# A linear-attention and RWKV block: another order at the start, for the woven tiles and between the two parts

## The chip, the cores and the metric

The kernel runs on one core of a Trainium2 chip. The metric is the device time of one execution in microseconds, as the median of several runs. A core has TensorE (PE in the profile), VectorE (DVE), ScalarE (ACT), GpSimd (POOL) and SyncE (SP), each with an instruction stream of its own that it works through in order; they wait for each other through semaphores. SP does nothing here but issue DMAs. ScalarE issues some as well.

## What is computed

The input x has 16 sequences of 1024 rows with 512 columns, in float32. The block has two parts, each with a residual and a layer norm:

```python
x = layernorm(x + attention(x)); x = layernorm(x + ffn(x))
# attention: 16 heads of 32
q, k, v = split(x @ Wqkv.T + bqkv)
qf, kf = relu(rope(rmsnorm(q, gq))), relu(rope(rmsnorm(k, gk)))
vk  = einsum('bhlp,bhld->bhpd', [v, 1], kf)      # a sum over a whole sequence
res = einsum('bhpd,bhld->bhlp', vk, qf)
out = rmsnorm((res[..., :-1] / (res[..., -1:] + eps)) @ Wout.T + bout, gout)
# ffn: x_prev is x shifted down one row within the sequence
r = sigmoid((mu_r*x + (1-mu_r)*x_prev) @ W_r.T)
k = square(relu((mu_k*x + (1-mu_k)*x_prev) @ W_k.T))
out = r * (k @ W_v.T)
```

The q side of a row can be finished only when vk of its sequence is known.

## The kernel before

Work goes by tiles of 128 rows: N = 128 tiles, eight to a sequence. Every float32 operand of a product is split into a rounded high part (a copy on ScalarE) and the rest (a subtraction on VectorE or GpSimd), and each product is three matmuls: high by high, high by low, low by high. A tile's projection to q is therefore 12 matmuls of 128x512 (four chunks of 512 by three).

**First part.** `slot(i)` (L566) is called for i = 0 to N-1. It issues the load of xt two tiles ahead (L568), the projections of tile i to q and k (`proj`, L367), the splits of the next tile (`split_x`, `split_xn`), the product of k and x of the tile before (`add_kx`, L452, 12 matmuls into four PSUM banks that gather a whole sequence), `rope` (L420: VectorE multiplies both projections by tables, ScalarE sums their squares, POOL takes the root at L120, then k is rectified and split), the tables for the next tile (`tables`, L397: POOL makes the first eight tiles' tables from g_qk, cos and sin and SP stores them; later tiles load them), and `seed` (L385: ScalarE copies the bias into the PSUM banks of the next projections). PSUM has eight banks: four gather k and x, and four are handed out in turn by `bank` (L96) to everything else, so a new user of a bank waits for the fourth user before it.

Once in eight slots a sequence is closed: `finish_a` (copies the four banks out), `finish_s` (column sums of k), `finish_b` (products with the v weights, 16 + 16 small matmuls, then the mask), `finish_c` (product with Wout, which gives a matrix m for the sequence that is stored as m_d). In slots i with i mod 8 = 1 stand finish_a and finish_s, in 2 finish_b, in 3 to 6 one finish_c each.

**Woven tiles.** The first NPRE = 7 tiles' q side is taken into the first part: from slot FIRST = 40, one tile every STEP = 8 slots. In slot FIRST + 8j the tile's q and x are loaded (the first one also the matrix m of its sequence); `part_s` (L217) seeds its bank with the output bias. One slot later come `part_q` (L189, six VectorE operations that normalise q), and for the first NT = 4 tiles `part_qt` (transposes q on TensorE and splits it), `part_m` (product with m, 12 matmuls) and `part_y` (L245: norms and residual on VectorE, ScalarE and POOL).

**Late weights.** `late_weight` (L553) loads one of 20 blocks of weights, splits it and, for the second part's weights, stores the halves. The code calls it once a slot from slot 1, but nothing ties it there.

**Between the parts** (L685 to L728): the first mixes of the second part, the q side of tiles 4 to 6, the closing of the last sequence, weights' loads and the q side of tiles 7 and 8. **Second part** (L781): for each half sequence s (four tiles), `part_t` transposes and mixes, `part_fk`, `part_fr` and `part_fv` are the three products, and the q side of later tiles is taken in, one each u.

**What sets the order.** The program's order is not the order on the engines. The framework (`TileContext(..., schedule_with_timeline_sim=True)`, L878) plans each engine's order by a simulation of its own: what it takes to be ready goes first, and the program's order breaks ties. `tc.issue_after(ins)` holds what is issued in its block on the same engine behind `ins`; it waits for nothing. Memory comes from pools; a pool that is opened after another was closed takes its memory and waits for the last use of what it overlaps.

Of the kernel before, what the change touches and what calls it, by code (L numbers as in the profile page):

```python
# [15 lines left out]
P = 128  # L16
# [6 lines left out]
FIRST, STEP = 40, 8  # L23
# [10 lines left out]
def kernel(  # L34
# [70 lines left out]
    const.tile([P, 40], F32, name="fill_const")  # L105
    tp.tile([P, 56], F32, name="fill_top")
    halo = const.tile([P, NC_], F32, name="halo")
    ident = const.tile([P, P], F32, name="ident")
    make_identity(nc, ident)
    rstd_all = const.tile([P, N, 2], F32, name="rstd_all")  # L110
# [146 lines left out]


    with ExitStack() as a_ctx:
# [50 lines left out]

        m0 = te.tile([P, 2, DIM], F32R, tag="m", bufs=2, name="m0")
        V.memset(f32(m0[:, 0, :]), 0.0)
        for n in range(8):
            T.matmul(bank(f"pswarm{n}"), lhsT=m0[:, 0, 0:P], rhs=m0[:, 0, :], start=True, stop=True)
        load_xt(0)
        split_x(0)
        b_qk = ca.tile([P, 2 * DIM], F32, name="b_qk")
        nc.scalar.dma_start(out=b_qk, in_=bqkv[0 : 2 * DIM].partition_broadcast(P))
        for j in range(2):
            cols = slice(j * DIM, (j + 1) * DIM)  # L320
            for c in range(NC_):
                n = NC_ * j + c
                split_w(
                    w_qk["h"][:, c, cols],
                    w_qk["l"][:, c, cols],
                    wqkv[:, c, cols],
                    (V, G)[c % 2],
                    (nc.sync, nc.scalar)[c % 2],
                    *(("x", XA), ("q", 3))[n >= XA],
                )  # L330
        load_xt(1)
        load_xn(0)
        g_qk = wp.tile([P, 2 * DIM], F32, tag="m", bufs=NC_, name="g_qk")
        nc.scalar.dma_start(out=g_qk, in_=gqk.partition_broadcast(P))
        cos = ca.tile([P, 8, HH], F32, name="cos")
        nc.scalar.dma_start(out=cos, in_=cos_t)
        sin = ca.tile([P, 8, HH], F32, name="sin")
        nc.scalar.dma_start(out=sin, in_=sin_t)

        sn = ca.tile([P, 8, 2, HH], F32, name="sn")  # L340
        G.tensor_copy(sn[:, :, 0, :], sin)
        G.tensor_scalar(sn[:, :, 1, :], sin, -1.0, None, ALU.mult)
        nc.scalar.dma_start(out=b_out, in_=bout.partition_broadcast(P))
        nc.scalar.dma_start(out=g_out, in_=gout.partition_broadcast(P))
        mu, omm = {}, {}
        for n, m in (("k", mu_k), ("r", mu_r)):
            mu[n] = const.tile([P, NC_], F32, name=f"mu_{n}")
            nc.scalar.dma_start(out=mu[n], in_=m)
            omm[n] = const.tile([P, NC_], F32, name=f"omm_{n}")
            V.tensor_scalar(omm[n], mu[n], -1.0, 1.0, ALU.mult, ALU.add)  # L350

        bv = te.tile([P, 64], F32, name="bv")[:, 0:NC_]
        with nc.allow_non_contiguous_dma(reason="512 numbers"):
            nc.scalar.dma_start(
                out=bv, in_=bqkv[2 * DIM : 3 * DIM].rearrange("(g p) -> p g", p=P)
            )

        mask = te.tile([P, P], BF16, name="mask")
        V.memset(mask, 0.0)
        for h in range(P // DH):  # L360
            V.memset(mask[h * DH : (h + 1) * DH, h * DH : (h + 1) * DH], 1.0)
        ones = te.tile([P, P], F32R, name="ones")
        V.memset(f32(ones), 1.0)
        state = {}
        ps_kx = {}

        def proj(i, j):  # L367

            ps = first.pop((i, j))
            cols = slice(j * DIM, (j + 1) * DIM)  # L370
            for c in range(NC_):
                for n, (a, b) in enumerate(((xh, "h"), (xh, "l"), (xl, "h"))):
                    T.matmul(  # L373
                        ps,
                        lhsT=a[i][:, c, :],
                        rhs=w_qk[b][:, c, cols],
                        start=False,
                        stop=(c == NC_ - 1 and n == 2),
                        skip_group_check=True,
                    )  # L380
            return ps

# [14 lines left out]
        def tables(i):  # L397
# [4 lines left out]
            for j in range(2):  # L402
                for n in range(2):
                    tb = wa.tile([P, DIM], F32, tag=f"tab{j}{n}", name=f"tab{j}{n}{i}")
                    tab[i, j, n] = tb
                    if i >= 8:
                        nc.sync.dma_start(out=tb, in_=tab_d[t][:, j, n, :])
                        continue
                    g = g_qk[:, j * DIM : (j + 1) * DIM]
                    if n == 0:  # L410
                        c = cos[:, t, :].unsqueeze(1).to_broadcast([P, 2 * HEADS, HH])
                        G.tensor_mul(rows(tb), rows(g), c)
                    else:
                        c = sn[:, t, :, :].unsqueeze(1).to_broadcast([P, HEADS, 2, HH])
                        G.tensor_mul(halves(tb), halves(g), c)
                    nc.sync.dma_start(out=tab_d[t][:, j, n, :], in_=tb)

# [34 lines left out]
        def add_kx(i):  # L452
# [9 lines left out]
            for c in range(NC_):  # L462
                cols = slice(c * P, (c + 1) * P)
                for n, (a, r) in enumerate(((h, kh), (h, kl), (l, kh))):
                    T.matmul(  # L465
                        ps_kx[b][c],
                        lhsT=a[:, cols],
# [29 lines left out]
        def finish_b(b):  # L497
# [4 lines left out]
            for g in range(NC_):  # L502
# [4 lines left out]
                for c in range(NC_):  # L507
# [16 lines left out]
                kv = te.tile([P, P], F32, tag="kv", bufs=1, name=f"kv{b}{g}")  # L524
                V.scalar_tensor_tensor(
                    kv, ks[:, cols], bv[:, g : g + 1], ps[:, 0:P], ALU.mult, ALU.add
                )
                V.tensor_add(kv, kv, ps[:, P : 2 * P])
                V.tensor_mul(kv, kv, mask)
                S.copy(th[:, g, :], kv)  # L530
                V.tensor_sub(tl[:, g, :], kv, f32(th[:, g, :]))
# [31 lines left out]
        tables(0)  # L563
        seed(0)

        def slot(i):  # L566
            if i + 2 < N:
                load = load_xt(i + 2)  # L568
            b, t = divmod(i - 2, 8)
            if i - 2 >= 0 and t == 7:  # L570
                finish_a(b)
            if i < N:
                qk = [proj(i, 0), proj(i, 1)]
            if i + 1 < N:
                split_x(i + 1)
            if i < N:
                split_xn(i)
            if i + 1 < N:
                load_xn(i + 1)
            if i - 2 >= 0 and t == 7:  # L580
# [3 lines left out]
            if i - 11 >= 0 and (i - 11) % 8 < NC_ and i < N:  # L584
                finish_c((i - 11) // 8, (i - 11) % 8)
            if 0 <= i - 1 < N:
                add_kx(i - 1)
            if i < N:
                state[i] = rope(i, qk)
            if i + 1 < N:  # L590
                tables(i + 1)
                seed(i + 1)
            if 1 <= i and late and i < N:
                late_weight()
            j, late_by = divmod(i - FIRST, STEP)
            if 0 <= j < NPRE:
                if late_by == 0:
# [7 lines left out]
                    if j < NT:  # L605
                        part_s(j)
                if late_by == 1:
                    part_q(j)
                    if j < NT:
                        part_qt(j)  # L610
                        part_y(j, part_m(j))
# [7 lines left out]
        wm = ctx.enter_context(tc.tile_pool(name="workm", reuse_waits="tile", bufs=1))  # L619
        w_f = {}  # L620
# [46 lines left out]
        def part_fk(s, o):  # L667
# [10 lines left out]
            kh = wm.tile([P, HT], F32R, tag="kah", bufs=5, name=f"kah{s}{o}")  # L678
            kl = wm.tile([P, HT], F32R, tag="kal", bufs=5, name=f"kal{s}{o}")
# [6 lines left out]
        for j in range(NT, NPRE):  # L686
            part_s(j)
        for c in range(NC_):
            turn(0, c)
            mix_t(0, c, "k")  # L690
        slot(N)
        for j in range(NT, NPRE):
            part_qt(j)
            part_y(j, part_m(j))
        slot(N + 1)
        part_fk(0, 0)
        part_fk(0, 1)
        slot(N + 2)
        part_fk(0, 2)
        part_fk(0, 3)  # L700
        tk_ctx.close()
        tx_ctx.close()
        wb = ctx.enter_context(tc.tile_pool(name="workb", reuse_waits="tile", bufs=1))
        wr = ctx.enter_context(tc.tile_pool(name="workr", reuse_waits="tile", bufs=1))
        own["ks"] = wr
        load_w("r", wr)
# [3 lines left out]
        )  # L710
        for g in range(NC_):
            finish_c(NB - 1, g)
        for c in range(NC_):
            turn(0, c)
            mix_t(0, c, "r")
        early = range(NPRE, 2 * NT + 1)
        load_ks(1)
        for j in early:
            load_q(j)
        load_q(2 * NT + 1)  # L720
        ps_m = {}
        for j in early:
            if j < 2 * NT:
                part_s(j)
            part_q(j)
            part_qt(j)
            if j < 2 * NT:
                ps_m[j] = part_m(j)  # L728
# [5 lines left out]
    def part_fr(s, t):  # L734
# [7 lines left out]
        gate[s, t] = wr.tile([P, DIM], F32, tag="gate", bufs=4, name=f"gate{s}{t}")  # L742
# [31 lines left out]
    for j in early:  # L774
# [3 lines left out]
    for j in ps_m:  # L778
        part_y(j, ps_m[j])
    load_w("v", wc)  # L780
    for s in range(NH):  # L781
# [100 lines left out]
```

## Time and profile before

| | us |
|---|---|
| median of 3 runs | 2780.74 (2779.46 to 2781.07) |
| the profiled execution | 2783.15 |
| its span, first to last instruction | 2781.3 |
| first matmul of a projection starts | 17.82 |
| last matmul of the first part's projections (tile 127) starts | 1226.3 |
| TensorE busy | 2706.2 |
| ScalarE busy | 1887.7 |
| mean granted TensorE clock | 0.989 |

Page and answers give times in microseconds and means in nanoseconds. A row of a group reads: line, engine, operation, output and inputs by the program's names, shape, count, busy time, mean. PE busy is drawn from modelled ends of pipelined matmuls. Of two engines' waits, "A <- B" names what ended the wait.

### The profile page before, as it was taken

To read this page: it belongs to the slowest core of one execution; us is meant where nothing else is said; L and a number is where in the kernel's file an instruction comes from. 1 tells how busy PE (TensorE), PEld (TensorE's weight loads), DVE (VectorE), ACT (ScalarE), POOL (GpSimd) and SP (SyncE) were. 2 spreads that over 40 slices of the span, in tenths; PEclk is the share of its full clock that TensorE was granted. 3 is DMA by queue.
4 is the path that set the end of the run, shared out by engine and by line. 5 is a ranking of instruction groups with operands and counts; after the bars stand their busy time and mean duration, and the time that the engine had idled before them with its cause. 6 is when DMAs were issued, how large, how long until landed. Compare 5 with 4: busy or idle time off the path is not lost.

```text
span 2781.3 us, 40329 instructions
## 1 busy us (share of the span) xinstructions
PE 2706.2 (97%) x12536; PEld 2237.5 (80%) x12536; DVE 2197.8 (79%) x4966; ACT 1887.7 (68%) x3839; POOL 737.0 (26%) x808
## 2 busy tenths in 40 slices
PE   7999999999999999988999999999999999999998
PEld 5788877777888888876788888888888888888887
DVE  7888877777888888866778787878787878788774
ACT  5566655555555665655777777777777777777775
POOL 6422221222222222222422222222222222222221
PEclk9999999999999999999999999999999999999999
DMA  7787786666777777755323323332323132323210
GB/s 251 230 296 254 242 258 202 214 201 203 233 239 239 241 239 237 231 184 178 93 82 96 105 71 97 95 110 65 107 91 114 57 112 86 110 66 107 76 58 31
DMA packets 230854, 431.17 MB, mean 155 GB/s; under 512 B 24544, under 2 KB 24800, under 8 KB 230640
## 3 DMA queue, kind: packets, MB, share of 16 engines
q1 hardware_dynamic: 228384, 425.85, 48.4%
q10 hardware_dynamic: 2256, 2.76, 0.4%
q8 instruction: 99, 1.62, 0.2%
q14 instruction: 115, 0.94, 0.1%
HBM read 313.14 MB, written 115.38 MB: 154 GB/s over the span
## 4 chain that ended last, share of the span: by engine, by line
PE 73%; DVE 1%; DMA 1%; ACT 1%; issue 0%; SPq 0%; POOL 0%; POOLq 0%; ACTq 0%
PE psk L156 13%; PE psv L156 12%; PE psr L156 12%; PE psy L156 12%; PE pskx L465 6%; PE psq L373 6%; PE psk L373 6%; PE pst L141 2%; PE psqt L141 2%; PE psm L541 1%; PE pskv L508 1%; DMA m_d<-m 0%; DMA w_r<-w_dr 0%; PE pskv L516 0%; DMA x<-in_x_dram 0%
## 5 line engine op out<-in xcount | busy, mean ns | idle before, releaser
L156 PE MATMUL psk<-mkh,w_k 128*128 128x512 f32 x1024 | 336.4, 395 | 0.0
L156 PE MATMUL psr<-w_r,mrh 128*128 128x512 f32 x1024 | 324.3, 398 | 2.6 <-issue 2.6
L156 PE MATMUL psv<-w_v,kah 128*128 128x512 f32 x1024 | 322.9, 396 | 1.5 <-DVE qtl L212 1.5
L156 PE MATMUL psy<-mb,qth 128*128 128x512 f32 x1024 | 317.4, 391 | 3.4 <-ACT qth L211 2.8
L120 POOL TENSOR_TENSOR rstd_all<-ss,mhalf 128x2 f32<-128x2 f32 x128 | 120.4, 940 | 678.3 <-DVE ss L435 646.6
L373 PE MATMUL psq<-wqk_h,xh 128*128 128x512 f32 x512 | 204.9, 400 | 26.4 <-ACT psq L135 26.4
L248 DVE TENSOR_TENSOR y<-psy,g_out 128x512 f32<-128x512 f32 x128 | 88.3, 690 | 179.5 <-PE psy L156 179.5
L156 PEld LDWEIGHTS psy<-mb,qth 128*128 128x128 f32 x1024 | 192.6, 189 | 44.7 <-ACT qth L211 3.9
L156 PEld LDWEIGHTS psk<-mkh,w_k 128*128 128x128 f32 x1024 | 192.4, 188 | 38.8
L156 PEld LDWEIGHTS psr<-w_r,mrh 128*128 128x128 f32 x1024 | 188.9, 189 | 39.7 <-issue 2.8
L156 PEld LDWEIGHTS psv<-w_v,kah 128*128 128x128 f32 x1024 | 188.5, 189 | 38.2 <-DVE qtl L212 1.9
L652 POOL TENSOR_TENSOR mkl<-mixk,mkh 128x512 fp32r<-128x512 f32 x128 | 176.2, 1376 | 149.3 <-ACT mkh L651 149.3
L465 PE MATMUL pskx<-kl,xnh 128*128 128x512 f32 x512 | 201.7, 394 | 4.9 <-DVE kl L442 4.8
L373 PE MATMUL psq<-wqk_l,xh 128*128 128x512 f32 x512 | 203.3, 397 | 0.0
L373 PE MATMUL psq<-wqk_h,xl 128*128 128x512 f32 x512 | 203.1, 397 | 0.0
L373 PE MATMUL psk<-wqk_h,xh 128*128 128x512 f32 x512 | 199.9, 390 | 1.8 <-ACT psk L135 1.8
L156 PE MATMUL psr<-w_r,mrl 128*128 128x512 f32 x512 | 201.3, 393 | 0.0
L156 PE MATMUL psv<-w_v,kal 128*128 128x512 f32 x512 | 200.5, 392 | 0.0
L156 PE MATMUL psy<-mb,qtl 128*128 128x512 f32 x512 | 200.1, 391 | 0.0
L465 PE MATMUL pskx<-kh,xnl 128*128 128x512 f32 x512 | 199.9, 391 | 0.0
L156 PE MATMUL psk<-mkl,w_k 128*128 128x512 f32 x512 | 199.8, 390 | 0.0
L373 PE MATMUL psk<-wqk_h,xl 128*128 128x512 f32 x512 | 199.4, 389 | 0.0
(148 smaller groups left out, 7246.1 us busy)
## 6 DMA issues: line engine op xcount, KB each, us to landing
tab<-tab_d SPq DMA_DIRECT2D x480, 256.0 KB
xt<-in_xt_dram SPq DMA_DIRECT2D x128, 256.0 KB
xn<-in_x_dram SPq DMA_DIRECT2D x128, 256.0 KB
q_d<-ro SPq DMA_DIRECT2D x128, 256.0 KB
m_d<-m SPq DMA_DIRECT2D x64, 512.0 KB
mb<-m_d SPq DMA_DIRECT2D x64, 512.0 KB
q<-q_d SPq DMA_DIRECT2D x128, 256.0 KB
x<-in_x_dram SPq DMA_DIRECT2D x128, 256.0 KB
```

The source lines that it names most:

```text
L120: G.tensor_tensor(dst, src, mhalf[:, 0 : src.shape[1]], ALU.pow)
L141: T.matmul(ps[:, n * P : (n + 1) * P], lhsT=b, rhs=ident, is_transpose=True, start=(n == 0), stop=(n == NC_ - 1), skip_group_check=True,)
L156: T.matmul(ps, lhsT=a[u][:, rows], rhs=b[w][:, cols], start=(afresh and c == 0 and k == 0), stop=(c == n - 1 and k == 2), skip_group_check ...
L248: V.tensor_mul(y, ps, g_out)
L373: T.matmul(ps, lhsT=a[i][:, c, :], rhs=w_qk[b][:, c, cols], start=False, stop=(c == NC_ - 1 and n == 2), skip_group_check=True,)
L465: T.matmul(ps_kx[b][c], lhsT=a[:, cols], rhs=r, start=(t == 0 and n == 0), stop=(t == 7 and n == 2),)
L508: T.matmul(ps, lhsT=w_a["h"][:, c, cols], rhs=kx[:, c, g, :, :].rearrange("p two n -> p (two n)"), start=(g % 2 == 0 and c == 0), stop=Fal ...
L541: T.matmul(ps, lhsT=a[:, g, :], rhs=w_o[r][:, g, :], start=(n == 0), stop=(n == 2))
L652: (V if n == "r" and s != 1 else G).tensor_sub(ml, m, f32(mh))
```

## The change

- Two new or changed constants: FIRST goes from 40 to 46, and NDONE = 4 names the number of woven tiles whose q side is done in the first part. A woven tile's steps are spread: loads in slot FIRST + 8j, part_q and part_qt in the next, part_s, part_m and part_y in the one after.
- At the beginning the casts of the q half of the weights, seed(0), the loads of g_qk, cos and sin and tables(0) come before the k half; all the low halves are made on VectorE (GpSimd made four of eight). The table that rope needs first is made first. The loads of b_out, g_out, mu_k, mu_r and bv go from ScalarE's queue at the start to SP's in slot 2, behind that slot's load of xt.
- Late weights begin in slot 5 instead of 1, each behind the load of xt in its slot.
- add_kx takes the four banks in turn for each of its three factors and the one with kl last.
- finish_b works on two groups at a time after the first step.
- Between the parts the order is another: both weights are loaded first, each of tiles 4 to 6 is seeded just before its product, with the closing steps of the last sequence among them, then the first mixes. slot(N) to slot(N + 2) are gone and their steps are written out. Tile 7 and part_fk(0, o) come after the pools are changed. Pieces of memory move between pools (`kah`, `kal`, `gate`; w_r; fill tiles).

```diff
-FIRST, STEP = 40, 8
+FIRST, STEP = 46, 8
+NDONE = 4
+    def rest(j):
+        part_s(j)
+        part_qt(j)
+        return part_m(j)
...
         load_xt(0)
-        split_x(0)
         b_qk = ca.tile([P, 2 * DIM], F32, name="b_qk")
         nc.scalar.dma_start(out=b_qk, in_=bqkv[0 : 2 * DIM].partition_broadcast(P))
+        split_x(0)
...
-                    (V, G)[c % 2],
+                    V,
...
+            if j == 0:
+                seed(0)
+                nc.scalar.dma_start(out=g_qk, in_=gqk.partition_broadcast(P))
+                nc.sync.dma_start(out=cos, in_=cos_t)
+                nc.sync.dma_start(out=sin, in_=sin_t)
+                G.tensor_copy(sn[:, :, 0, :], sin)
+                G.tensor_scalar(sn[:, :, 1, :], sin, -1.0, None, ALU.mult)
+                tables(0)
         load_xt(1)
         load_xn(0)
...
-            for c in range(NC_):
-                cols = slice(c * P, (c + 1) * P)
-                for n, (a, r) in enumerate(((h, kh), (h, kl), (l, kh))):
+            for n, (a, r) in enumerate(((h, kh), (l, kh), (h, kl))):
+                for c in range(NC_):
...
-            if 1 <= i and late and i < N:
-                late_weight()
+            if i == 2:
+                with tc.issue_after(load.ins):
+                    constants()
+            if i >= 5 and late:
+                with tc.issue_after(load.ins):
+                    late_weight()
             j, late_by = divmod(i - FIRST, STEP)
...
-                    if j < NT:
-                        part_s(j)
                 if late_by == 1:
                     part_q(j)
-                    if j < NT:
+                    if j < NDONE:
                         part_qt(j)
-                        part_y(j, part_m(j))
+                if late_by == 2 and j < NDONE:
+                    part_s(j)
+                    part_y(j, part_m(j))
...
         load_w("k", cb)
-        for j in range(NT, NPRE):
-            part_s(j)
-        for c in range(NC_):
-            turn(0, c)
-            mix_t(0, c, "k")
-        slot(N)
...
+        load_w("r", cb)
+        load_ks(1)
+        y5 = rest(NDONE)
+        add_kx(N - 1)
+        part_y(NDONE, y5)
         tk_ctx.close()
+        finish_a(NB - 1)
         pa_ctx.close()
...
+        part_y(NDONE + 1, rest(NDONE + 1))
+        finish_s(NB - 1)
+        finish_b(NB - 1)
+        first = 2 * NT
+        tx_ctx.close()
+        wb = ctx.enter_context(tc.tile_pool(name="workb", reuse_waits="tile", bufs=1))
+        for c in range(NC_):
+            part_t(0, c)
+        part_y(NDONE + 2, rest(NDONE + 2))
+        for j in range(NPRE, first + 2):
+            load_q(j)
         for g in range(NC_):
             finish_c(NB - 1, g)
...
-    for j in early:
+    for j in range(NPRE, first + 1):
         load_x(j)
     for c in range(NC_):
         load_m(1, c)
-    for j in ps_m:
-        part_y(j, ps_m[j])
+    for j in range(NPRE, first):
+        part_q(j)
+        part_y(j, rest(j))
+    for o in range(NC_):
+        part_fk(0, o)
     load_w("v", wc)
+    part_q(first)
+    part_qt(first)
```

## The prediction

> **What bounds the kernel now.** I read the page first: engine shares, the slices with the granted clock, and the chain.
>
> ```profile
> PE 2706.2 (97%) x12536; PEld 2237.5 (80%) x12536; DVE 2197.8 (79%) x4966; ACT 1887.7 (68%) x3839; POOL 737.0 (26%) x808
> PE   7999999999999999988999999999999999999998
> PEclk9999999999999999999999999999999999999999
> PE 73%; DVE 1%; DMA 1%; ACT 1%; issue 0%; SPq 0%; POOL 0%; POOLq 0%; ACTq 0%
> ```
>
> TensorE (PE) is the bound: 97% busy, and hardly anything else is on the chain. The change removes no matmul, so it can only win back time in which PE stood still or ran at half clock. Then the table of stretches (length, busy time by engine with instruction counts, granted clock, DMA share, GB/s) shows where that is:
>
> ```profile
> 0.00:50.00 50.00, 34.32 (x128) 25.88 (x128) 33.65 (x49) 27.48 (x55) 29.94 (x28) 0.86 0.85 279
> 50.00:100.00 50.00, 43.06 (x175) 33.60 (x176) 46.84 (x53) 23.23 (x48) 41.61 (x30) 0.97 0.59 198
> 100.00:200.00 100.00, 95.99 (x439) 78.11 (x439) 85.10 (x150) 64.57 (x136) 22.03 (x20) 1.00 0.87 287
> 400.00:700.00 300.00, 280.82 (x1258) 231.01 (x1257) 225.28 (x439) 168.43 (x364) 62.64 (x62) 0.97 0.67 207
> 700.00:1200.00 500.00, 500.00 (x2315) 417.98 (x2313) 412.11 (x743) 301.07 (x650) 115.47 (x104) 1.00 0.76 236
> 1200.00:1350.00 150.00, 128.20 (x575) 101.71 (x574) 100.72 (x231) 92.90 (x183) 45.43 (x47) 0.94 0.49 161
> 1350.00:2700.00 1350.00, 1350.00 (x6403) 1121.52 (x6403) 1092.21 (x2910) 1038.65 (x2055) 357.27 (x459) 1.00 0.29 90
> ```
>
> Two stretches have a full PE at full clock and can give nothing; the start, the woven stretch and the passage between the parts are not full. To size them I took the start of every matmul from the timeline and subtracted the ordinary start-to-start spacing of its shape (0.227 us for 512 columns, 0.171 for 256, 0.060 for 128, 0.109 for a transpose). The 12536 matmuls need 2665 us; the excess is 107 us: **35.8** in 0 to 200, **31.2** in 400 to 700, **34.0** in 1200 to 1350, 6 elsewhere. It holds idle time and slow-clock time. The waits of PE name the causes (total, times, longest):
>
> ```profile
> PE psq L373 <- ACT psq L135: 26.4, 8, 12.8
> PE pskx L465 <- ACT kh L441: 9.1, 6, 2.3
> PE pskx L465 <- DVE kl L442: 4.8, 7, 1.5
> ```
>
> A projection waits for the bias copy that seeds its PSUM bank: once at the start (12.8), most of the rest among the woven tiles.
>
> **Woven tiles.** Of the 16 sequences' closing products, finish_a and finish_s stand in slots i = 1 mod 8, finish_b in 2, finish_c in 3 to 6. FIRST = 40 puts part_q, part_qt, part_m and part_y in slots 1 mod 8. VectorE's load: 412.1 of 500 us is 59.5 per eight slots of 72.2 us (a kx group recurs every 72.2); closing rows (42.3 + 43.6 + 41.8 + 21.8 + 18.3 + 17.9 + 10.8 = 196.5 us over 16 sequences) are 12.3, so a plain slot is 5.9. A woven tile adds 5.8: part_q 2.85 (365 us of its six rows / 128), qtl 0.69, y 0.69, the x update 0.83, small ones 0.7. Slots 1 and 2 now hold 11.8 + 9.6 (finish_a, s, b) + 5.8 = 27.2 us of VectorE beside 16.3 (72 projections and kx) + 0.45 + 3.7 + 3.16 = 23.6 of PE: overloaded, 115%. After: part_q and part_qt fall in slot 7, part_s, part_m and part_y in slot 0: 17.6 beside 16.3 + 3.16 = 19.5, 90%, and one extra PSUM bank a slot, as finish_c's slots have without a stall. The tiles' loads (q, x, and once ks and four m, 2.9 MB) move six slots with them on SP, past nothing that waits for them: 0. Four tiles lose 31.2 now, about 7 each (11.5 the first). I leave 1 us a tile for a slot 7 that alone is overfull (5.9 + 3.5 against 8.6) and count **-27** (bounds -15: half stays; -31). The rule of "TensorE: Matmul & The Clock Gate" (Part 1: The HAM clock gate) is that only an idle stretch over about 3.4 us drops the clock. By it the first tile alone (idle 3.5) would pay for slow matmuls, and the other stalls cost idle time only. The timeline shows half-speed matmuls (0.43 apart) after a 2.0 us gap at 431.5 too, so I take the excess with its clock part, 31.2; by the rule it would be some 28.
>
> **Start.** The timeline of ScalarE before the first projection:
>
> ```profile
> 14.37 1.14 ACT L307 CAST wqk_h<-wstage 128x512 fp32r<-128x512 f32 x2 [1.53 <-DMA g_qk<-in_gqk_dram]
> ...
> 16.75 0.39 ACTq L354 DMA_DIRECT2D bv<-in_bqkv_dram  x1
> 17.18 0.59 ACT L135 COPY psq<-b_qk 128x512 f32<-128x512 f32 x1 [1.67 <-DMA b_out<-in_bout_dram]
> ```
>
> The seed at 17.18 stands behind eight weight casts and eight DMA triggers (g_qk to bv); the change moves five (the constants) to slot 2 on SP and two (cos, sin) to SP's start. Four casts (the q half) were over at 10.4. With seed(0) behind these four, PE can begin near 10.5 instead of 17.8; the k half's last cast was at 15.5, while 12 cold matmuls last till 15, so no new wait follows. That is 7 us for the first matmul, but not yet for slot 8: in 40 to 100 the slots last 9.3 us (36 matmuls: 8.2), since VectorE is 94% and POOL 83% busy. POOL builds 32 tables (mean 1.69 and 1.51 us there), and VectorE's operations with two SBUF inputs (ro L430) take 1.22 us instead of 0.68. What counts is how much sooner the tables end: POOL began them at 16.8 and stood 3.2 + 3.6 us waiting for a rope that was behind eight subtractions of wa and wout on VectorE (mean about 1.1). These go to slots 5 to 12, POOL loses four wqk_l (1.3 each), VectorE gains four (0.69, by 12, when it is half idle: hidden; uncovered they'd cost 2.8). I take 9 us sooner (5 to 14). Against it: wa's four subtractions now fall among the tables. The row's median is 0.68; "SBUF — State Buffer" (Who interferes with whom) holds that a VectorE operation with two SBUF inputs is blocked for the whole of a GpSimd operation[...]. By the row they cost 2.7, by the rule 7.1 (4 x the 1.78 that ro's slow ones show); the row's mean in that stretch, 1.22, gives 4.9. VectorE is bound there, but wa and wout leave it earlier, so I charge 2. add_kx with kl last moves the need of kl back by four matmuls, 0.9 us a time for 7 waits: 1 credited, since the seeds come late next. Sum **-8** (0 to -15). The other late weights (12) were already at 105 to 222 and stay near there; the constants' five triggers on SP (0.33 each, 1.7 us) stand ahead of slot 3's loads, hidden by a slot of 9 us; uncovered, 1.7. Moved along with tables(0): its four stores and cos, sin now come before xt(1) and xn(0) on SP, six triggers of 0.4 or 2.4 us, and 1.1 MB, 4 us at the 279 GB/s of the first row. xt(1) is needed when psq(1) starts, near 18, and was triggered at 7.5: hidden; uncovered it costs those 4 us, which the low end takes in.
>
> **The waits that are added.** Each late load now stands on SP behind the load of xt two slots on, and its cast on ScalarE waits for it. Behind that cast are the seeds and kh, for which PE waits. The nearest rows are ScalarE's waits for such DMAs now (wk 2.9, wr 4.0, wv 3.5 us once each). Low bound 0 (ScalarE is 60% busy), high bound 20 x 3 us; I take 0, since in 100 to 200 these waits are there and the excess is only 6.
>
> **Between the parts.** Three seeds (psy 4 to 6) are placed in three of four banks ahead of the transposes, so that turn(0, c) goes round in one bank; w_r waits for finish's memory. Longest pieces of the chain here:
>
> ```profile
> 1276.22 8.22 DMA w_r<-w_dr
> ...
> 1284.50 9.41 DMA m_d<-m
> ...
> 1299.49 7.54 DMA x<-in_x_dram
> ```
>
> After: seeds come one at a time; rest(4) beside kx 126 fills the 5.2 us in which kh(127) is made (1226.3 to 1231.5); w_r is loaded with w_k from 1227 (8 x 0.5 MB at the 256 GB/s of its 8.22 us: 16 us, before the mixes are done); eight banks are there for the transposes. Work up to the end of part_fk(0): PE 86 x 0.227 + 4 x 3.16 + 3.7 + 1.7 = 38 us; ScalarE 14.7 (four tiles at 3.69) + 10.4 (mixes) + 7.4 (fk) + 9.5 = 42; VectorE about 41. So ScalarE, not PE, sets it: at least 4 us stay. m_d, then x7 and m(1) still follow finish_c through the same memory (9.4 + 7.5), but rest(7), fk and fr (3.2 + 10.9 + 10.9) lie over them: 5. The loop of s = 0 keeps its order: 5 lost at 1312 to 1345, by the same count. Remaining 14 of 34: **-20** (-8 to -28). Pairs in finish_b save VectorE some 0.6 us a sequence where PE is full: 0. Fill tiles, w_r and gate in other pools: no instruction; 0 either way unless a reused tile holds a load, which is in the range.
>
> **Sum.** The profiled execution took 2783.15 (span 2781.3, 1.85 around it): 2783.15 - 27 - 8 - 20 = 2728.2; the median of the runs is 2.4 below the profiled one, so **2726**.
>
> **Rivals.** (1) The weave's stalls only move: slots 7 and 0 stall as 1 did, because VectorE is in order and slot 7 is overfull. For it: 9.4 against 8.6. Against: part_q of tiles 4 to 6 stands in the busier slot 1 in 700 to 1200 without any loss. Time 2726 + 22 = 2748; 10%. (2) The passage stays ScalarE-bound with its short chains and no fk to fill: 28 of 34 remain, 2740; 15%. (3) Everything fits and only 25 us of the 101 remain: 2705; 8%. (4) Slower: the tied loads. If each of 20 casts holds ScalarE so long that the next seeds are late by 3 us, 60 us are added and 55 won: 2786. It decides from 2.75 us a weight; against it speak the 100 to 200 row and that wstage has seven buffers; 3%. (5) The planner that orders each engine keeps its old order at the start (the seed still behind the casts): 2734, 10%. The likeliest, 54%, is 2726.
>
> **Range.** 2706 to 2749: it takes in (1), (2) and (5) and the terms' ends partly added. A measurement of this kernel tells about 0.2% (5.6 us) from no change. Faster 0.94, same 0.03, slower 0.03.
>
> **What would show it.** Weave: no psq wait between 400 and 700, kx groups 75.4 us apart, clock 1.00. Start: first psq near 10.5, tables over near 88. Between: no 8 us w_r piece on the chain, 1200 to 1350 with PE near 140 busy. Wrong it would be if the casts of late weights show waits in slots 5 to 24 with psq waiting behind, or if ScalarE's DMA triggers still stand before the first seed.

## The result and the profile after

The kernel after took **2747.9 us** (median of 4 runs, 2744.3 to 2751.2) against 2780.9 for the kernel before beside it: a ratio of 0.988, 95% interval 0.9865 to 0.9899. 33 us were won where 55 had been forecast. The profiled execution took 2751.16 (span 2749.4).

The page of the kernel after: TensorE's share, its slices, and the chain by engine.

```profile
PE 2698.3 (98%) x12520; PEld 2227.0 (81%) x12520; DVE 2197.8 (80%) x4874; ACT 1878.3 (68%) x3807; POOL 724.5 (26%) x804
PE   8899999999999999998999999999999999999998
PE 66%; DVE 11%; issue 5%; DMA 5%; ACT 4%; POOL 1%; SPq 0%; DVEq 0%; ACTq 0%; POOLq 0%
```

The matmuls are 16 fewer (12536 before): the mixes' transposes of the first half sequence are now made once and not twice, which is 1.7 us at 0.109 each. TensorE has less of the chain than before (66 for 73%) and VectorE more, though the kernel is faster. The table of stretches of the kernel after (same columns as before):

```profile
0.00:50.00 50.00, 38.26 (x137) 28.55 (x138) 40.24 (x52) 25.24 (x50) 31.89 (x29) 0.93 0.72 229
50.00:100.00 50.00, 44.13 (x179) 33.58 (x178) 44.15 (x54) 24.22 (x52) 35.18 (x27) 0.97 0.60 210
200.00:400.00 200.00, 198.27 (x904) 163.59 (x903) 163.35 (x276) 120.89 (x258) 44.59 (x42) 1.00 0.79 255
400.00:700.00 300.00, 296.23 (x1366) 246.90 (x1365) 241.40 (x438) 181.56 (x382) 67.08 (x66) 0.99 0.75 237
700.00:1200.00 500.00, 495.95 (x2282) 411.17 (x2281) 406.43 (x700) 294.97 (x633) 112.61 (x104) 1.00 0.73 230
1200.00:1350.00 150.00, 136.24 (x641) 109.92 (x640) 117.22 (x281) 104.88 (x209) 52.87 (x57) 0.99 0.44 145
1350.00:2700.00 1350.00, 1350.00 (x6390) 1120.17 (x6389) 1081.55 (x2876) 1037.51 (x2050) 351.47 (x453) 1.00 0.28 89
```

400 to 700 went from 280.8 busy to 296.2, 1200 to 1350 from 128.2 to 136.2. New is that 200 to 400 and 700 to 1200, which were full, now miss 1.7 and 4.1. With the prediction's own measure (start-to-start time over the ordinary spacing of each shape) the excess, which is the time that TensorE lost, is in us:

| traced execution | 0–100 | 100–200 | 200–400 | 400–700 | 700–1150 | 1150–1350 | rest |
|---|---|---|---|---|---|---|---|
| before | 29.8 | 6.0 | 0.0 | 31.2 | 0.0 | 34.0 | 5.8 |
| after | 27.2 | 5.2 | 3.3 | 6.5 | 7.3 | 19.8 | 7.3 |
| b_weave | 30.5 | 4.0 | 0.0 | 4.9 | 6.1 | 33.3 | 5.8 |
| b_kx | 30.0 | 7.4 | 1.6 | 31.3 | 3.0 | 32.5 | 5.9 |
| a_notab | 16.1 | 6.5 | 2.1 | 7.2 | 8.2 | 18.6 | 7.5 |
| a_late1 | 23.8 | 5.2 | -0.1 | 5.4 | 7.8 | 19.1 | 7.7 |
| a_late1kx | 25.2 | 4.9 | 0.0 | 8.1 | 6.2 | 19.4 | 7.7 |

Before to after: 0 to 200 won 3.4, the woven stretch 24.7, the passage 14.2, the transposes 1.7; 3.3 + 7.3 + 1.5 were lost in stretches that had lost nothing or little. The sum is 31.9, and the two profiled executions differ by 32.0, so nothing is unaccounted for. The 1.5 in the last stretch is no property of the change: five of the traces of the a_ runs below lose 2.2 less there than after does.

What TensorE waited for over the whole kernel after (total, times, longest):

```profile
PE pskx L477 <- ACT kh L454: 10.3, 9, 2.4
PE pskx L477 <- DVE kl L455: 4.3, 6, 1.0
PE pskv L520 <- DVE kv L538: 4.2, 4, 2.5
PE psq L421 <- ACT wqk_h L313: 2.7, 1, 2.7
PE psq L421 <- ACT psq L136: 2.6, 6, 0.7
```

The wait for the seeds, 26.4 before, is 2.6; its place is not taken by another seed; kh (the cast of the rectified k) now leads, with 10.3 for 9.1 before.

The start on ScalarE, after, in order of time:

```profile
6.19 0.58 ACT L136 COPY psq<-b_qk 128x512 f32<-128x512 f32 x1
...
7.31 0.62 ACT L313 CAST wqk_h<-wstage 128x512 fp32r<-128x512 f32 x1
...
13.04 1.25 ACT L313 CAST wqk_h<-wstage 128x512 fp32r<-128x512 f32 x2 [2.23 <-DMA wstage<-in_wqkv_dram]
```

The seed stands ahead of the first weight cast, and the first projection starts at 7.98 (before 17.82). The k half's casts then wait 2.23 us for their load, ahead of which those of g_qk (on ScalarE's queue), cos and sin (on SP's) now stand, and TensorE waits 1.3 us at 14.35 and 1.3 at 16.12 for the casts and their low halves.

### The profile page after: what moved, and what is told of

Its sections match the earlier page's. It is cut to its first block, busy times and chain, and to the rows that moved or that the text cites. A ratio compares the mean times of both kernels' runs of the same rounds, so it can differ in the third digit from the quotient of the medians.

```text
span 2749.4 us, 40113 instructions
## 1 busy us (share of the span) xinstructions
PE 2698.3 (98%) x12520; PEld 2227.0 (81%) x12520; DVE 2197.8 (80%) x4874; ACT 1878.3 (68%) x3807; POOL 724.5 (26%) x804
## 4 chain that ended last, share of the span: by engine, by line
PE 66%; DVE 11%; issue 5%; DMA 5%; ACT 4%; POOL 1%; SPq 0%; DVEq 0%; ACTq 0%; POOLq 0%
PE psk L157 13%; PE psr L157 12%; PE psv L157 12%; PE psy L157 12%; PE pskx L477 4%; PE psq L421 4%; PE psk L421 3%; DVE ro L442 3%; DVE t L441 2%; PE pst L142 2%; PE psqt L142 2%; DMA q_d<-ro 2%; DVE ro L443 2%; DMA q<-q_d 1%; DVE kl L455 1%
## 5 line engine op out<-in xcount | busy, mean ns | idle before, releaser
L121 POOL TENSOR_TENSOR rstd_all<-ss,mhalf 128x2 f32<-128x2 f32 x128 | 111.1, 868 | 682.7 <-DVE ss L448 651.9
L421 PE MATMUL psk<-wqk_l,xh 128*128 128x512 f32 x512 | 200.1, 391 | 1.3 <-DVE wqk_l L314 1.3
L136 ACT COPY psk<-b_qk 128x512 f32<-128x512 f32 x128 | 75.8, 593 | 161.2 <-DVE ro L442 159.0
```

The costliest lines, as they stand in the source:

```text
L121: G.tensor_tensor(dst, src, mhalf[:, 0 : src.shape[1]], ALU.pow)
L136: S.copy(ps, src)
L421: T.matmul(ps, lhsT=a[i][:, c, :], rhs=w_qk[b][:, c, cols], start=False, stop=(c == NC_ - 1 and n == 2), skip_group_check=True,)
```

## The experiments

The theory after the result was: the three places that were repaired gave most of what was forecast, and the shortfall is in what was put down as costing nothing, namely slot 7 (where the program now has part_q of tiles 4 to 6), the new order in add_kx, the tied late weights, and the chains of ScalarE and VectorE in the passage. The rival: the repairs themselves gave less, since tables, loads or pairs set the pace. Names with b_ are the kernel before with one part added, those with a_ the kernel after with one part taken back or changed. All times, with the ratio to before on the same chip:

| run | us (lowest to highest) | ratio, 95% |
|---|---|---|
| b_weave | 2763.1 (2760.8–2764.0) | 0.9935 (0.9919–0.9952) |
| b_kx | 2788.5 (2786.2–2791.2) | 1.0028 (1.0020–1.0037) |
| a_oldkx | 2745.0 (2744.9–2745.5) | 0.9870 (0.9855–0.9884) |
| a_oldkv | 2749.1 (2744.2–2752.5) | 0.9883 (0.9867–0.9899) |
| a_q1 | 2749.8 (2746.3–2752.3) | 0.9890 (0.9875–0.9905) |
| a_spread | 2750.0 (2745.5–2753.1) | 0.9888 (0.9871–0.9904) |
| a_late8 | 2755.1 (2751.2–2756.4) | 0.9908 (0.9893–0.9922) |
| a_xearly | 2754.0 (2751.8–2755.9) | 0.9906 (0.9891–0.9920) |
| a_notab | 2747.3 (2740.4–2754.0) | 0.9886 (0.9869–0.9902) |
| a_tab01 | 2747.4 (2741.9–2752.7) | 0.9878 (0.9860–0.9895) |
| a_late1 | 2747.6 (2743.0–2749.7) | 0.9876 (0.9862–0.9891) |
| a_late1kx | 2746.7 (2745.3–2752.3) | 0.9885 (0.9870–0.9900) |

Executions of one a_ kernel spread over 0.6 to 14 us, and I take it that medians of four tell no two of them apart by under some 4 us. Traces spread as well: in the twelve traces with the new weave (after, b_weave and the ten a_ runs) 400 to 700 loses 3.0 to 9.1 and 700 to 1150 loses 5.4 to 8.2, also where nothing in that stretch was changed. A gain of a few microseconds in one trace belongs to that execution.

**b_weave: the weave alone, in the kernel before.**

```diff
-FIRST, STEP = 40, 8
+FIRST, STEP = 46, 8
...
-                    if j < NT:
-                        part_s(j)
...
-                        part_y(j, part_m(j))
+                if late_by == 2 and j < NT:
+                    part_s(j)
+                    part_y(j, part_m(j))
```

> The kernel before with the woven tiles alone moved (FIRST = 46, steps spread over two slots), nothing else. Theory W (the stalls of 400 to 700 are VectorE's overload in slots 1 and 2, and the move alone removes them): about 25 us faster than before, some 2756, and 700 to 1200 stays without a stall. Rival P (the planner's new order for the moved steps is what costs the 7.4 us in 700 to 1200 of the changed kernel): 25 us won and 5 to 10 given back, 2762 to 2766, with PE below 500 of 500 us in 700 to 1200.

It won 17.7 us. Two rows of the table of stretches of b_weave:

```profile
400.00:700.00 300.00, 296.57 (x1372) 246.75 (x1372) 241.65 (x460) 183.18 (x394) 67.69 (x65) 1.00 0.74 235
700.00:1200.00 500.00, 496.46 (x2287) 412.17 (x2287) 407.68 (x747) 297.89 (x648) 117.19 (x104) 1.00 0.74 232
```

The woven stretch is repaired as forecast (26.3 of 31.2 won), and 6.1 are given back after 700, where only the end of tile 3 and the loads and part_q of tiles 4 to 6 have moved. Most of the 7.3 that after loses there comes with the weave and needs nothing else of the change.

**b_kx: the new order in add_kx alone, in the kernel before.**

```diff
-            for c in range(NC_):
-                cols = slice(c * P, (c + 1) * P)
-                for n, (a, r) in enumerate(((h, kh), (h, kl), (l, kh))):
+            for n, (a, r) in enumerate(((h, kh), (l, kh), (h, kl))):
+                for c in range(NC_):
```

> The kernel before with add_kx's new order alone (factor outside, bank inside, kl last). Theory K (this order is what brings the new small stalls in 200 to 400 and 700 to 1200): 5 to 11 us slower than before, 2786 to 2792, with psq waits in 700 to 1200. Rival (the order only moves the need of kl back, as predicted): 0 to 3 us faster, 2778 to 2781, and PE full in 700 to 1200.

It is 7.7 us slower. The prediction had credited 1 for a later need of kl. The traced execution lost 1.6 in 200 to 400 and 3.0 in 700 to 1150, where nothing was lost before, and 1.4 more in 100 to 200. Why the order costs this no run here settles. One reading, argued only: after a sequence's last tile finish_a can take the first of the four banks only when all are near their end, since each bank gets its last matmul in the final four. The waits over 0.5 us that TensorE has in those two stretches are for kh (0.9 at 816.9 and at 890.4) and kl (1.0 at 203.6), none for finish_a's copies, so the reading would have to work through these.

**a_oldkx: the kernel after with the old order in add_kx** (the diff of b_kx reversed).

> The changed kernel with add_kx's old order put back. Theory K: 5 to 11 us faster than the changed kernel, some 2739, with PE full from 200 to 1200. Rival: 0 to 3 us slower than the changed kernel, since kl waits come back in 30 to 130.

Its median is 2.9 us under after's, but after's lowest run (2744.3) lies below it. In 700 to 1150 it lost 5.6, in 200 to 400 2.9. So the new order is no gain shown in after either, and it isn't what made the two full stretches leak.

**a_oldkv: the kernel after with finish_b's steps one group at a time, as before.**

```diff
-                if g % 2 == 1:
-                    two = slice(g - 1, g + 1)
...
+                V.tensor_add(kv, kv, ps[:, P : 2 * P])
+                V.tensor_mul(kv, kv, mask)
+                S.copy(th[:, g, :], kv)
+                V.tensor_sub(tl[:, g, :], kv, f32(th[:, g, :]))
```

> The changed kernel with finish_b's old single steps put back (one group at a time). Theory V (the paired steps hold the bank longer, so pskv waits for kv and slot 2 stalls; 4.2 us of such waits in the changed kernel): 3 to 6 us faster than the changed kernel. Rival (pairs only spare VectorE and ScalarE instructions): 0 to 4 us slower than the changed kernel.

No difference (2749.1 for 2747.9, with 6.6 lost in 700 to 1150): the theory that the pairs cause the loss falls, and the prediction's 0 for the pairs stands.

**a_q1: part_q of tiles 4 to 6 back in a slot 1.**

```diff
-                if late_by == 1:
+                if late_by == (1 if j < NDONE else 3):
                     part_q(j)
-                    if j < NDONE:
-                        part_qt(j)
+                if late_by == 1 and j < NDONE:
+                    part_qt(j)
```

> The changed kernel with part_q of tiles 4 to 6 alone put back into slots 1 mod 8 (late_by == 3); tiles 0 to 3 stay spread over slots 7 and 0. Theory Q (part_q in an overfull slot 7, 5.9 + 2.9 against 8.2 us, carries a lag of VectorE into slot 1, where finish_a and finish_s come on top): the stalls after slots 87 and 95 (near 860 and 934, two of the 7 us in 700 to 1150) go, 2 to 5 us faster than the changed kernel, and what is left lies at tiles 0 to 3. Rival (the planner's order is different anyway, the place of part_q doesn't matter): no change within 2 us, stalls near 860 and 934 stay.

Before asking what moved, look at how such a stall looks in after, on ScalarE:

```profile
854.27 0.19 ACT L438 ACTIVATION_READ_ACCUMULATOR junk<-psk 128x1 f32 x1
859.13 0.72 ACT L451 ACTIVATE ro<-ro,rstd_all 128x512 f32<-128x512 f32 x1 [4.67 <-DVE ro L443]
859.76 0.58 ACT L136 COPY psq<-b_qk 128x512 f32<-128x512 f32 x1
```

ScalarE stands 4.67 us for rope's ro, and the seed of the next projection is planned behind it; TensorE starts that projection at 860.39, 0.66 late. One such stall at 834.62 (0.8) follows part_q of tile 5, whose steps lie among VectorE's others from 825 to 830, after 2.1 us in which VectorE waited for the tile's q. So one would expect a_q1 to show what part_q's place is worth. But part_q did not move. Its first operation, for all seven tiles (count, shortest, median and longest ns, first and last start), in after:

```profile
L194 DVE SCALAR_TENSOR_TENSOR pr<-q,ksb x7: 691/693/694, 453.7 to 900.4; 128x512 f32<-128x512 f32 x7
```

and in a_q1:

```profile
L194 DVE SCALAR_TENSOR_TENSOR pr<-q,ksb x7: 692/693/798, 454.6 to 901.4; 128x512 f32<-128x512 f32 x7
```

Tiles 4 to 6 start at 750.7, 825.3 and 900.4 in after, at 752.1, 826.0 and 901.4 in a_q1, though the program calls them two slots later there. The planner takes the step at the same place. So this run says nothing of part_q's place. The stall at 834 is gone all the same, that at 860 shrinks from 0.7 to 0.3, those at 910 and 935 stay; 700 to 1150 falls from 7.3 to 5.7, 400 to 700 rises from 6.5 to 9.1, and the time doesn't move.

**a_spread: a woven tile over four slots.**

```diff
-FIRST, STEP = 46, 8
+FIRST, STEP = 44, 8
...
                 if late_by == 1:
                     part_q(j)
-                    if j < NDONE:
-                        part_qt(j)
-                if late_by == 2 and j < NDONE:
+                if late_by == 3 and j < NDONE:
+                    part_qt(j)
+                if late_by == 4 and j < NDONE:
```

> The changed kernel with each woven tile spread over four slots: loads in slot 4, part_q in 5, part_qt in 7, part_s, part_m and part_y in 0 (FIRST = 44). Theory Q: VectorE has slots 6 and 7 to work off part_q before slot 1, so the stalls of 400 to 700 (6.5) and of 700 to 1150 (7.3) shrink to 5 or less together: 5 to 9 us faster than the changed kernel. Rival: slot 5 holds a finish_c as well (5.9 + 0.7 + 2.9 against 8.9) and stalls in its place: within 3 us.

TensorE's waits from 400 to 760 in a_spread:

```profile
PE pskv L520 <- DVE kv L538: 4.2, 4, 1.3
PE psk L421 <- ACT psk L136: 2.2, 2, 1.2
PE psm L557 <- DVE m L560: 1.9, 1, 1.9
```

The program now calls part_q in a slot with a finish_c, and a wait of 1.9 us for m comes up; 9.0 are lost in 400 to 700. But a_q1, whose tiles 0 to 3 are woven as in after, lost 9.1 there. So a thinner spread is no gain, and whether it costs anything isn't shown.

**a_late8: the late weights from slot 8.**

```diff
-            if i >= 5 and late:
+            for _ in range(2 if i in (8, 9) else 1 if i >= 10 and late else 0):
                 with tc.issue_after(load.ins):
                     late_weight()
```

> The changed kernel with the late weights two a slot in slots 8 and 9 and one a slot from 10, so that none falls among POOL's tables. Theory L (the start won only 3.4 of 8 because wa's loads, casts and subtractions in slots 5 to 8 hold ScalarE 5.8 us and VectorE 3.8 us in order while the tables are made): 0 to 100 loses 4 to 6 us less, so 3 to 6 us faster than the changed kernel, if slots 8 to 10 take two weights without a stall. Rival (POOL's tables and the lock-step with rope set the pace there, wa only fills gaps): 0 to 100 within 1.5 us of the changed kernel's 27 us of excess.

It is 7 us slower, and 50 to 100 lost 13.2 instead of 9.8: the first late weight is cast at 91.2, when the last table is made, and the stage got no faster. The splits of wa aren't what slows it.

**a_xearly: x of tiles 7 and 8 loaded before finish_c, into other memory.**

```diff
         for j in range(NPRE, first + 2):
             load_q(j)
+        for j in range(NPRE, first + 1):
+            load_x(j)
```

(their x tiles are taken from workb there, and the later load_x is dropped). The longest transfer in the chain of the kernel after between 1200 and 1350:

```profile
1258.03 8.48 DMA x<-in_x_dram
```

> The changed kernel with x of tiles 7 and 8 loaded earlier, into a pool that is free once the last finish_b is over (two of the four inner x tiles lie in workb), not after the last m_d stores. Theory M (the chain of x, 8.5 us at 1258 to 1266.5, sets the stalls of 1257 to 1300, 10.7 us): 4 to 7 us faster than the changed kernel. Rival (ScalarE and VectorE, with about 42 us of work each beside 38 of TensorE, and their in-order waits set it): within 2 us, and the waits for part_q's q and for the r and qtl stay.

The piece is gone from the chain and nothing is won: the median is 6 us above after's, 22.5 are lost in 1150 to 1350, and the same stalls stand there as in after, 2.0 us before the product of tile 4, 1.3 before fr, 3.7 (after: 3.0) before tile 8's transposes. The first two wait for ScalarE (the casts qth and the rectified r), the third for part_q of tile 8 on VectorE. A transfer that the chain names was hidden all the same. Of the traced execution's 4.8 us over after's, 2.7 lie in the passage and 3.4 in the first 200 us, which the edit doesn't touch, so what makes this kernel slower is open.

**a_notab: no tables made after the first tile's.**

```diff
-            t = i % 8
-            if i < 8:
+            t = 0
+            if i < 1:
...
-                    if i >= 8:
+                    if i >= 1:
```

> The kernel after, but only tile 0's tables are made; tiles 1 to 7 load tile 0's tables from memory as the later tiles load theirs (so seven tiles of each sequence turn with the wrong angles: the work left out is 28 table products on GpSimd and their stores). Theory T: in the first 100 us GpSimd's tables and VectorE's operations with two SBUF inputs hold each other up, so that a slot lasts 10.0 us instead of the 8.2 that 36 matmuls need. Without the tables the slots of 30 to 100 last about 8.5, the excess of PE from 50 to 100 goes from 9.8 to under 4, and the time falls by 6 to 14 us to 2734 to 2742. Rival: the weight loads (DMA is 60 to 85% busy) or the late weights' splits set the pace; then the slots stay near 10.0, the excess stays near 9.8 and the time is within 3 us of 2748.

GpSimd's longest wait in the kernel after between 25 and 97 (total, times, longest):

```profile
POOL tab L348 <- DVE t L441: 9.6, 7, 1.8
```

It waits for VectorE's use of the last table before it can make the next in its place. The stretch 50 to 100 in the table of a_notab:

```profile
50.00:100.00 50.00, 45.39 (x196) 35.96 (x194) 33.07 (x57) 26.83 (x57) 9.43 (x9) 1.00 0.68 216
```

Without the tables VectorE is busy for 33.1 of 50 us instead of 44.2, the products of k and x of tiles 0 and 7 start 59.1 us apart instead of 70.1 (8.4 a slot, 8.5 expected), 0 to 200 lost 22.6 instead of 32.4, and that execution took 2740.4, as the theory had it. So the tables, by their work and this mutual wait together, do set the pace of the first 100 us. But a stall of 4.0 for kh comes up at 103, and the median, 2747.3, isn't lower: the other three executions took 2747 to 2754. The stage is explained; that removing it shortens the kernel isn't shown.

**a_tab01: the cosine table first, as before.**

```diff
-                for n in (1, 0):
+                for n in range(2):
```

> The kernel after with the cosine table of a tile made before the sine table, as before the change. In the trace of after, GpSimd waited seven times, 9.6 us in all, to start a sine table until VectorE had used the old one. Theory O: the order of the tables is what made the slots of the table phase 10.0 us long instead of 9.5; with the old order GpSimd's wait falls to under 5 us, the tables end 3 us or more sooner and the time falls by 3 to 4 us to 2744. Rival: the order only decides which table waits; the pace comes from the total of both engines' work and stays 10.0, the time within 2 us of 2748, or longer by 1 to 2 since rope's first multiplication starts later in slot 0.

No difference in the time (2747.4), and 50 to 100 lost 12.7: the order of the tables isn't the cause.

**a_late1: late weights untied and from slot 1.**

```diff
-            if i >= 5 and late:
-                with tc.issue_after(load.ins):
-                    late_weight()
+            if 1 <= i and late:
+                late_weight()
```

> The kernel after with the late weights from slot 1 and tied to no load, as before the change. Theory D: the tie and the later start moved the twenty weights' casts and subtractions into 200 to 400, which lost nothing before and 3.3 us after (with a wait of 1.7 for kh at 253.7); untied, 200 to 400 falls under 1 us, and what was gained at the start (3.4 us in 0 to 200) goes back only in part, so the time is 2744 to 2748. Rival: the early weights crowd the table phase again (wa's casts and subtractions in slots 1 to 5): 0 to 200 grows by 3 to 8 us, the time is 2750 to 2755.

In the kernel after, ScalarE's last weight casts run like this:

```profile
242.36 0.19 ACT L438 ACTIVATION_READ_ACCUMULATOR junk<-psq 128x1 f32 x1
246.21 0.62 ACT L313 CAST wv<-wstage 128x512 fp32r<-128x512 f32 x1 [3.66 <-DMA m_d<-m]
...
253.04 0.61 ACT L454 CAST kh<-ro 128x512 fp32r<-128x512 f32 x1
```

The cast stands 3.66 us for a DMA, everything behind it on ScalarE is late, kh at 253.04 too, and TensorE waits 1.70 us for kh at 253.70. In a_late1 the last such cast is at 214. The stretch 200 to 400 in the table of a_late1:

```profile
200.00:400.00 200.00, 200.00 (x918) 166.88 (x917) 164.46 (x282) 122.52 (x262) 44.57 (x41) 1.00 0.76 240
```

It is full again; it was not in any of the nine traces with the tied weights, which lose 2.0 to 6.0 there. 0 to 200 didn't grow but fell by 3.4. The mechanism is shown. The median (2747.6) doesn't show the gain.

**a_late1kx: both taken back, late weights and add_kx.**

> The kernel after with two parts of the change taken back: the late weights untied and from slot 1 (in whose trace 200 to 400 lost nothing and 50 to 100 lost 6.5 instead of 9.8) and the old order of the twelve matmuls in add_kx (whose time was 2745.0). Theory: the two add, excess in 0 to 200 near 28, in 200 to 400 under 1, in 700 to 1150 near 5.6, time 2740 to 2744. Rival: the early weights' gain is only one execution's chance (its median stayed at 2747.6 though its traced execution took 2743.0) and with the old order in add_kx the product waits in one bank at a time again: 2745 to 2748.

200 to 400 is full in this trace also, 0 to 200 lost 30.1, and the time is 2746.7: the rival holds. No kernel here is shown to beat the one after.

## Why the prediction was right in part

**Direction: right. Main term: right in its size, and only in part in its working.** The weave was to give 27 and gave 24.7 (26.3 by itself). Of the signs named, no psq wait of any length is left in 400 to 700 and the granted clock is 0.99; the closing sums of k come at intervals of 75.9, 80.2, 76.1 and 75.9 us where 75.4 were forecast (82 to 86 before). b_weave shows that the place of the woven tiles made the stalls. The prediction's reason, 27.2 us of VectorE in two slots against 23.6 of TensorE, is not what the engines did. It counted by the program's slots; in the trace before, part_q of tiles 1 to 6 starts some 18 us ahead of the closing sums of k and not behind them, and after 34 to 40 us ahead. VectorE in the slots 57 and 58 of the kernel before (tile 2, from one first psq matmul to the next):

```profile
564.60:578.10 13.50, 11.75 (x52) 9.18 (x51) 12.61 (x22) 10.21 (x24) 2.22 (x3) 1.00 0.64 196
578.10:595.20 17.10, 14.49 (x77) 12.19 (x76) 10.36 (x23) 7.08 (x16) 3.45 (x4) 1.00 0.42 133
```

Slot 57 is full, 12.6 of 13.5 us, and TensorE lost 2.1 there. In slot 58 it lost 3.0, and 1.7 more behind it at half clock (0.50 from 595.2 to 598.6), with VectorE busy for 10.4 of 17.1 us. There the engines wait for each other in order, as ScalarE shows at tile 1:

```profile
510.93 0.72 ACT L238 ACTIVATE junka<-x,nma 128x512 bf16<-128x512 f32 x1 [1.24 <-DVE nma L236]
...
512.36 0.59 ACT L135 COPY psq<-b_qk 128x512 f32<-128x512 f32 x1
```

The seed stands behind a square of part_y's norm that waits for VectorE, and TensorE, 2.0 us idle, starts the projection at 513.0. So that the sum came out near 27 is in part luck.

**Passage: mechanism right, size too large.** 14.2 for 20, and 1.7 more from the 16 transposes, which the sentence that the change removes no matmul had overlooked. The size doesn't hang on one execution: 1150 to 1350 loses 32.5 to 34.0 in the three traces of the old order and 18.2 to 20.9 in ten of the new. No run took a part of it back alone, so what each part gave isn't shown. The load of w_r has left the chain. The 5 us that the prediction left in the loop of s = 0 are still there in the main: from the first matmul of part_fv(0, 0) to the first of part_fk(1, 0) TensorE lost 5.0 before (from 1313.7) and 4.2 after (from 1277.9). What is left in after between 1200 and 1350 are waits for ScalarE's and VectorE's chains, as the second rival says, and not for transfers (a_xearly). The longest (total, times, longest):

```profile
PE psqt L142 <- DVE q L201: 3.3, 2, 2.9
PE psy L157 <- ACT qth L212: 3.1, 2, 1.9
PE pst L142 <- DVE mixr L657: 1.8, 1, 1.8
```

**Start: right in its cause, mis-sized by the tables.** The first projection came 9.8 us sooner (7 forecast), since the planner put the seed ahead of the casts; 2.5 of it went back in the new waits for the k half, where the prediction had seen none. The last table product, before and then after:

```profile
92.92 1.76 POOL L412 TENSOR_TENSOR tab<-g_qk,cos 128x512 f32<-128x512 f32 x1
...
89.41 1.81 POOL L345 TENSOR_TENSOR tab<-g_qk,cos 128x512 f32<-128x512 f32 x1
```

The tables end at 91.2 for 94.7, and 0 to 200 gained 3.4 for 8. The term that failed is 9 us sooner for the tables; it is 3.5. A slot there lasts 10.0 us, before 9.5 (products of k and x of tiles 0 and 7 start 70.1 us apart, 66.5 before). a_notab shows that the tables are what makes the slots long, a_late8 and a_tab01 that it is neither wa's splits nor the order. Why they are longer than before the traces say in part: with the late weights untied and from slot 1 it is 66.7 us in a_late1 and in a_late1kx, as before, and in the eight traces of tied weights in which the tables are made 68.9 to 71.3. So the later, tied weights lengthen the slots; by what way isn't shown.

The charge of 2 for wa's splits was near: three took 0.69 and one 1.08, 3.2 us in all against the 2.7 of the row and the 7.1 with all four held up. In the trace before it matters which of two operations starts first, VectorE's or GpSimd's:

```profile
39.53 0.69 DVE L430 TENSOR_TENSOR ro<-ro,t 128x512 f32<-128x512 f32 x1
39.63 1.76 POOL L412 TENSOR_TENSOR tab<-g_qk,cos 128x512 f32<-128x512 f32 x1 [0.18 <-POOL rstd_all L120]
...
42.74 1.63 POOL L412 TENSOR_TENSOR tab<-g_qk,cos 128x512 f32<-128x512 f32 x1 [0.56 <-POOL rstd_all L120]
43.13 1.79 DVE L430 TENSOR_TENSOR ro<-ro,t 128x512 f32<-128x512 f32 x1
```

Started 0.1 us ahead of a table product, ro takes 0.69; started 0.4 behind one, 1.79.

**The step that failed: "Two stretches have a full PE at full clock and can give nothing".** True, but the prediction charged them nothing either: 0 for part_q's move, 1 gained for add_kx, 0 for the tied weights. They lost 3.3 and 7.3, and the last stretch of this trace 1.5. That is 12.1 of the 23 us between forecast and profiled execution; the rest is start 4.6, passage 4.1 and weave 2.3. 200 to 400 is the tied weights (a_late1; the fourth rival at a twentieth of its size: one cast and one late kh make 1.7 of the 3.3, in place of 20 seeds). 700 to 1150 came with the weave (b_weave), as the first rival had it in kind. That rival's time, 2748, is the measured one by coincidence: it put 22 us on tiles 0 to 3, where 6.5 are left. How the 7.3 split among part_q's place, add_kx and rope's waits stays open: a_q1, a_oldkx and a_oldkv lost 0.7 to 1.7 less, but a_xearly, which changes nothing before 1150, also lost 1.7 less. The measured 2747.9 lies at the upper edge of the stated range, 2706 to 2749.

## What to carry to other kernels

A stretch in which the bounding engine is full has no cost today, but not for the next order of work: before putting 0 on a step moved into it, look how long the in-order engines behind it already wait there, and look in the trace where the planner puts the step, which need not be the slot that the program names. A load tied to a place in a queue is also a wait for the cast that uses it and for all that is planned behind that cast. And when executions spread by 7 us, several parts of 3 us can be read in traces, not proven in medians.

## What the runs showed that was not expected

- The same twelve matmuls in another order over four PSUM banks cost 7.7 us of 2780.8 (b_kx), with intervals that leave no doubt of the sign.
- One transfer of 8.48 us on the chain could be taken off it without gain (a_xearly), since VectorE's part_q ended as late beside it. Tile 8's transposes start 38.8 us behind the last closing sums in after and 39.4 in a_xearly.
- VectorE stands at each woven tile for its q: 7 times 2.2 us on the mean (15.2 in all; 20.4 before). The program puts part_q a slot behind the load, but from tile 1 on the planner takes it some 5 us behind the load's issue (tile 1 after: issued at 516.1, part_q at 520.9).
